# Query blocks of 496 and 351 columns, sixteen pairs weighted on GpSimd, and a new order of TensorE's work in a two-layer graph kernel

## The chip, the cores and the metric

The kernel runs on one core of a Trainium2 chip. The time is device microseconds of one launch. Engines are called as in the profile: PE is TensorE's matrix multiplication, PEld its loading of weights, DVE is VectorE, ACT is ScalarE, POOL is GpSimd, SP is the engine that issues most transfers.

## What is computed

3327 nodes with 128 channels pass two layers. Layer 0 is a graph convolution with a batch norm; layer 1, which takes nearly all of the time, is an attention that runs once for each of the 128 channels d:

```python
q = (x @ Wq.T).reshape(d, n, h)      # d = 128, n = 3327, h = 8
k = (x @ Wk.T).reshape(d, n, h)
v = (x @ Wv.T).reshape(d, n, h)
a = jnp.einsum('dnh,dmh->dnm', q, k) * scale
a = a + spatial_encoding + edge_encoding   # both are adj
a = jax.nn.softmax(a, axis=2)
out = jnp.einsum('dnm,dmh->dnh', a, v)
out = out.reshape(n, h * d)
return out @ Wo.T
```

So there are 128 attentions of 3327 queries against 3327 keys with only 8 features each, and the adjacency matrix is added twice to each score.

## The kernel before, in words

Everything is float32. Layer 0 and the preparation of layer 1 come first. Then the function `attention` works through 32 iterations (index `i`) of four channels each (`G = 4`). An iteration goes over the query blocks (index `y`), and each block over 13 steps (index `s`). Keys lie in 26 chunks of 128; a chunk is on the partitions and the queries of the block are the columns.

The unit of work is a pair: one chunk of keys and one half of the four channels, thus two channels. `product` (its matmul is L725) computes the scores of a pair with two matmuls of 32 rows each: the pair's half decides whether they use the first two or the last two of the array's four row groups. The result fills a tile `s` of two PSUM banks; there are three such tiles. A pair is then finished in one of two ways:

- plain: `add` on DVE (L818) adds the adjacency tile `at` into one of three places of `d`; later one exponential on ACT (L856) does all of `d`, issued one step later as `late`.
- weighted: `weighted` takes the exponential on ACT straight from PSUM (L828), and POOL multiplies it by exponentials of the adjacency values (L831, tile `wt`, read from the stored array `wd`).

A block has 52 pairs and each step handles four of them: three plain and one weighted in most steps, two and two in the last one. That makes 38 plain and 14 weighted pairs. `WC` is the first chunk that is weighted, and `pairs(s)` gives the pairs of a step.

The weights of the softmax are multiplied with v by `weigh` (L604): the stationary operand has 128 rows and 9 columns (8 features and a column of ones for the sum), and the two channels of a pair use two of the four column groups, again chosen by the half. This is done `LAG = 3` steps after the scores, by `second`. The program shows one such matmul as two instructions in the profile (two passes over the same columns). The output `av` takes one PSUM bank; there are two, in turns for the blocks.

All engines run in the order in which the program issues, so the order of calls in the loop over the steps is the order of TensorE's queue. Before, a step puts there: the score of the weighted pair, the score of the first plain pair, `second(0)` (pairs 0 and 1 of the old step), the scores of the other two pairs, and `second(1)` (pairs 2 and 3). `step()` moves on the end of a block, `finish`: a copy of `av` (L612), four transposes (L619), the division, the transfer to memory. `beside` puts in pieces of later or earlier work that use the other `av` bank: the projections of q, k and v for later channels (L196), two turns (L257) and a product (L265) of the output for earlier ones. `more_weights` prepares, in the first iteration only, the adjacency exponentials of the next blocks; the first `EARLY` blocks are prepared before the attention begins. `loads` fetches the next iteration's q, k and v, with a sorting copy on POOL (L180).

Of the kernel before, what the change touches and what calls it, by code (L numbers as in the profile page):

```python
# [18 lines left out]
N = 3327  # L19
# [3 lines left out]
NC = 26  # L23
T = N * D
NP = NC * P
NB = 512
G = 4
EPS = 1e-5
HALF = 0.5 / math.sqrt(D)
SAFE = 30.0  # L30
SU = NC // 2
WC = 19
CH = 4 * NP // D
NG = D // G
EARLY = 3

# [6 lines left out]
def tile_two_layer_gnn(  # L45
# [20 lines left out]
        mybir.EngineType.Pool, mybir.EngineType.SP,  # L66
    }))
    blocks = [(n0, min(NB, N - n0)) for n0 in range(0, N, NB)]

    const = ctx.enter_context(tc.tile_pool(name="const", bufs=1))  # L70
    dram = ctx.enter_context(tc.tile_pool(name="dram", bufs=1, space=DRAM))
# [42 lines left out]
    FROM = [3 * SU] + [LAG + 1] * (NG - 1)  # L114
# [171 lines left out]
    with tc.tile_pool(name="l0", bufs=1) as l0, tc.tile_pool(  # L286
# [125 lines left out]
        for c in range(NC):  # L412
# [16 lines left out]
            i = c - 2 * NQ - 5  # L429
            if 0 <= i < NQ - 2 and 4 * i + 4 <= c:  # L430
                spread(i)
        weights = []
        for y, (n0, w) in enumerate(blocks[:EARLY]):
            a = ap.tile([P, 7 * NB], F32, name="a")
            a7 = a.rearrange("p (c n) -> p c n", c=7)
            nc.sync.dma_start(a7[:, :, :w], adjr[:, WC:, n0 : n0 + w])
            weights.append((a7, n0, w))

# [170 lines left out]
    def finish(rp, av, d0, n0, w):  # L609

        avs = rp.tile([P, NB], F32, name="avs")
        nc.vector.tensor_copy(avs[:, :w], av[:, :w])  # L612
        yield

        J = 4 if w == NB else 3
        R = w // J
        pt = av.rearrange("p (j q) -> p j q", j=4)
        for j in range(J):
            nc.tensor.transpose(  # L619
                pt[:R, j, :], avs[:, j : j + (R - 1) * J + 1 : J], ident  # L620
            )
        yield
        pv = pt.rearrange("p j (b h) -> p b j h", h=32)
        ri = rp.tile([P, G, 4], F32, name="ri")

        nc.vector.tensor_scalar(ri[:R, :, :J], pv[:R, :, :J, H], 1e-30, None, ALU.max)  # L626
        nc.vector.reciprocal(ri[:R, :, :J], ri[:R, :, :J])  # L627
        o = rp.tile([P, G, 4, H], F32, name="oq")
        nc.vector.tensor_tensor(  # L629
            o[:R, :, :J, :],  # L630
            pv[:R, :, :J, :H],
            ri[:R, :, :J].unsqueeze(3).to_broadcast([R, G, J, H]),
            ALU.mult,
        )
        yield
        nc.sync.dma_start(
            attb[bass.ds(d0, G), n0 : n0 + w, :].rearrange(
                "b (p j) h -> p b (j h)", j=J
            ),
            o[:R, :, :J, :].rearrange("p b j h -> p b (j h)"),  # L640
        )
# [10 lines left out]
    def attention():  # L652


        with tc.tile_pool(name="adj", bufs=4) as ap, tc.tile_pool(
# [17 lines left out]
            if True:  # L673
                steps = [
                    (i, y, s)
                    for i in range(NG) for y in range(len(blocks)) for s in range(SU)
                ]

                def at(i):
# [2 lines left out]
                def pairs(s):  # L682


                    last = s == SU - 1
                    plain = [(j // 2, j % 2) for j in range(3 * s, 3 * s + 3 - last)]
                    rest = [(WC + s // 2, 1 - s % 2)]
                    return plain, rest + ([(NC - 1, 0)] if last else [])


                wanted, have = [], {}
                for x, (i, y, s) in enumerate(steps):
                    n0, w = blocks[y]
                    for c, _ in pairs(s)[0]:
                        if (0, i, y, c // 2) not in have:
                            have[0, i, y, c // 2] = None
                            wanted.append((x, 0, i, y, c // 2))
                    c = pairs(s)[1][0][0]
                    if (1, i, y, c) not in have:
                        have[1, i, y, c] = None  # L700
                        wanted.append((x, 1, i, y, c))

                def fetch(x):
                    while wanted and wanted[0][0] <= x:
                        _, kind, i, y, c = wanted.pop(0)
                        n0, w = blocks[y]
                        if kind:
                            a = wp.tile([P, NB], F32, name="wt")
                            nc.sync.dma_start(a[:, :w], wd[c - WC, :, n0 : n0 + w])
                        else:  # L710
                            a = ap.tile([P, 2, NB], F32, name="at")
                            n = min(2, WC - 2 * c)
                            nc.sync.dma_start(
                                a[:, :n, :w], adjr[:, 2 * c : 2 * c + n, n0 : n0 + w]
                            )
                        have[kind, i, y, c] = a

                def product(i, y, c, half):
                    q, k, _ = sets[i % 2]
                    n0, w = blocks[y]  # L720
                    we = w + w % 2
                    p = psc.tile([P, 2, NB], F32, name="s")
                    for x in range(2):
                        rs = slice(64 * half + 32 * x, 64 * half + 32 * x + 32)
                        nc.tensor.matmul(  # L725
                            p[:, x, :we], k[rs, c, :], q[rs, n0 : n0 + we],
                            start=True, stop=True,
                        )
                    return p
# [4 lines left out]
                def more_weights(i, y, s):  # L734

                    k, phase = s // 3, s % 3
                    if i or y + 1 >= len(blocks) or y + 1 < EARLY or k > 3:
                        return
                    n0, w = blocks[y + 1]
                    c = WC + 2 * k  # L740
                    n = min(2, NC - c)
                    if phase == 0:
# [13 lines left out]
                def beside(i, y, s):  # L756


                    for j in [1, 2] if i == 0 else [i + 2] if i + 2 < NG else []:
# [2 lines left out]
                        hj = wk.tile([P, CH], F32, name="hj")  # L762
                        nc.sync.dma_start(hj, hd[:, j * CH : (j + 1) * CH])
                        extra.extend(projections(wk, hj, j, False, ov, low_half[:CH, 1:2]))
                    if s in (8, 11) and extra:
                        drive(extra[0])
                    if s in (9, 12) and extra:
                        drive(extra.pop(0))
                    if s in (7, 10) and extra:
                        drive(extra[0], avs2[(i * len(blocks) + y + 1) % 2])  # L770
                    if (y, s) == (2, 12) and i:
                        extra.extend(outputs(wk, i - 1))

                extra = []

                def second(part):

                    (i, y, s), es = waiting[0]
                    n0, w = blocks[y]
                    av = avs2[(i * len(blocks) + y) % 2]  # L780
                    ps = sum(pairs(s), [])
                    for j in (0, 1) if part == 0 else (2, 3):
                        c, half = ps[j]
                        for x in range(2):
                            weigh(
                                sets[i % 2], av, w, es[j][:, x, :w], 2 * half + x, c,
                                s == 0 and part == 0, s == SU - 1 and part == 1,
                            )
                    if part:
                        waiting.pop(0)  # L790
                        if s == SU - 1:
                            ending.append(finish(rp, av, at(i), n0, w))

                def step():
                    for g in ending[:1]:
                        if next(g, g) is g:
                            ending.pop(0)

                for x, (i, y, s) in enumerate(steps):
                    n0, w = blocks[y]  # L800
                    fetch(x + PRE)
                    k = x - i * SU * len(blocks) - FROM[i]
                    if k == 0 and i + 1 < NG:
                        pending = loads(sets[(i + 1) % 2], at(i + 1))
                        total = len(pending)

                    while pending and (total - len(pending)) * (SU * len(blocks) - FROM[i] - 4) <= k * total:
                        pending.pop(0)()
                    more_weights(i, y, s)
                    due = len(waiting) == LAG  # L810
# [11 lines left out]
                            SAFE / 2, p[:, :, :w], ALU.min, ALU.add,  # L822
                        )

                    def weighted(c, half):
                        f = fp.tile([P, 2, NB], F32, name="f")
                        p = product(i, y, c, half)
                        nc.scalar.activation(  # L828
                            f[:, :, :w], p[:, :, :w], AF.Exp, scale=2.0
                        )  # L830
# [4 lines left out]
                        )  # L835
                        es.append(f)

                    weighted(*rest[0])
                    if late is not None:
                        late()  # L840
                    add(0, product(i, y, *plain[0]))
                    if due:
                        second(0)
                    step()
                    add(1, product(i, y, *plain[1]))
                    if len(rest) > 1:
                        weighted(*rest[1])
                    else:
                        add(2, product(i, y, *plain[2]))
                    beside(i, y, s)  # L850
                    if due:
                        second(1)

                    def late(d=d, w=w, n=len(plain)):
                        flat = d[:, :n].rearrange("p j x n -> p (j x) n")[:, :, :w]
# [1 line left out]

                    waiting.append(((i, y, s), es))
                late()
                while waiting:  # L860
                    second(0)
                    step()
                    second(1)
                while ending:
                    step()
                for p, b in zip(outputs(wk, NG - 1), (0, 1, 0)):
# [4 lines left out]
    def attention_shifted():  # L871

        with tc.tile_pool(name="shq", bufs=1) as shp, tc.tile_pool(
# [11 lines left out]
            with tc.For_i(0, D, G) as d0:  # L885
# [3 lines left out]
                for b in range(G):  # L889
# [1 line left out]
                        sh[32 * b : 32 * b + 1],  # L891
                        sT[:, bass.ds((d0 + b if b else d0) * N, N)],
                    )
                for y, (n0, w) in enumerate(blocks):
                    we = w + w % 2
                    av = avs2[y % 2]
                    waiting = []
# [166 lines left out]
```

## Time and profile before

| | |
|---|---|
| median of 3 runs | 10516.94 us (10514.26 to 10520.51) |
| profiled execution | 10527.91 us, its span 10526.1 us |
| mean granted TensorE clock | 0.986 |
| first score of the attention begins | 280.4 us after the span's start |
| iterations begin | 280.4, 667.9, 984.3, ... 5431.4, ... 9875.1, 10188.9 us |
| a steady iteration | 317.4 us (5431.4 to 9875.1, divided by 14) |
| DMA | 163 GB/s in mean; queue of the transfers busy 56.3% |

The times of instructions come from one profiled execution, and the span runs from its first to its last instruction. In the groups of instructions, a line gives the source line, the engine, the operation, the tiles (written<-read), the shapes and the count, then the busy time in us and the mean duration in ns of one, and then the idle time of the engine just before them and who ended it. In the waits, a line says who waited for whom, the total in us, the number of times and the longest. In the timeline the columns are the start and the duration in us; equal instructions that follow each other without a gap are merged to one row (xcount). A matmul row's duration reaches to its modelled end, and matmuls overlap in the array; the distance between starts is the better measure.

### The profile page before, as it was taken

To read this page: it belongs to the slowest core of one execution; us is meant where nothing else is said; L and a number is where in the kernel's file an instruction comes from. 1 tells how busy PE (TensorE), PEld (TensorE's weight loads), DVE (VectorE), ACT (ScalarE), POOL (GpSimd) and SP (SyncE) were. 2 spreads that over 40 slices of the span, in tenths; PEclk is the share of its full clock that TensorE was granted. 3 is DMA by queue.
4 is the path that set the end of the run, shared out by engine and by line. 5 is a ranking of instruction groups with operands and counts; after the bars stand their busy time and mean duration, and the time that the engine had idled before them with its cause. 6 is when DMAs were issued, how large, how long until landed. Compare 5 with 4: busy or idle time off the path is not lost. (4 is left out here: it accounts for less than half of the span.)

```text
span 10526.1 us, 186778 instructions
## 1 busy us (share of the span) xinstructions
PE 9922.7 (94%) x72399; PEld 2813.8 (27%) x72399; DVE 9714.9 (92%) x9949; ACT 9948.5 (95%) x6200; POOL 7497.1 (71%) x3868
## 2 busy tenths in 40 slices
PE   7889999999999999999999999999999999999999
PEld 3222222222222222222222222222222222222222
DVE  5789999999999999999999999999999999999998
ACT  4889999999999999999999999999999999999998
POOL 0667777777777777777777777777777777777776
PEclk8899999999999999999999999999999999999999
DMA  7655555555555555555555555555555555555554
GB/s 241 192 168 163 157 168 165 163 162 160 162 166 165 164 162 157 161 170 163 160 162 157 165 170 165 160 158 163 164 169 163 162 163 158 165 165 167 156 152 128
DMA packets 1115761, 1731.67 MB, mean 165 GB/s; under 512 B 198350, under 2 KB 441932, under 8 KB 1107180
## 3 DMA queue, kind: packets, MB, share of 16 engines
q1 hardware_dynamic: 1110478, 1713.99, 56.3%
q8 instruction: 568, 9.31, 0.4%
q10 hardware_dynamic: 4350, 5.64, 0.2%
q14 instruction: 333, 2.73, 0.1%
q0 software_dynamic: 32, 0.00, 0.0%
HBM read 1618.76 MB, written 100.53 MB: 163 GB/s over the span
## 5 line engine op out<-in xcount | busy, mean ns | idle before, releaser
L818 DVE SCALAR_TENSOR_TENSOR d<-at,s 128x1024 f32<-128x1024 f32 x8512 | 9204.3, 1138 | 642.7 <-PE s L725 406.2
L831 POOL TENSOR_TENSOR f<-f,wt 128x1024 f32<-128x1024 f32 (+1 forms) x3136 | 6983.8, 2235 | 2619.1 <-ACT f L828 2572.0
L856 ACT ACTIVATE d<-d 128x3072 f32<-128x3072 f32 (+1 forms) x2912 | 7372.9, 2532 | 73.4 <-DVE d L818 70.5
L604 PE MATMUL av<-d,v 128*9 128x512 f32 x34048 | 5528.5, 569 | 0.1
L725 PE MATMUL s<-q,k 32*128 32x512 f32 x23296 | 4280.7, 482 | 505.7 <-DVE d L818 218.0
L725 PEld LDWEIGHTS s<-q,k 32*128 32x128 f32 x23296 | 1773.9, 182 | 5829.2 <-DVE d L818 3312.2
L828 ACT ACTIVATE f<-s 128x1024 f32<-128x1024 f32 (+1 forms) x3136 | 3014.8, 970 | 313.8 <-PE s L725 252.3
L604 PE MATMUL av<-f,v 128*9 128x512 f32 x12544 | 2864.0, 571 | 0.0
L604 PEld LDWEIGHTS av<-d,v 128*9 128x9 f32 x34048 | 630.7, 88 | 1381.6 <-issue 1265.4
L604 PEld LDWEIGHTS av<-f,v 128*9 128x9 f32 x12544 | 310.6, 88 | 52.9 <-issue 41.0
L180 POOL CAST k<-ks 128x256 fp32r<-128x256 f32 x434 | 284.2, 655 | 0.0
L416 PE MATMUL acc<-a,A 128*128 128x512 f32 (+1 forms) x364 | 151.3, 568 | 24.0 <-ACT A L350 23.3
L619 PEld LDWEIGHTS av<-ident,avs 128*128 128x128 f32 (+1 forms) x864 | 121.1, 208 | 179.9 <-issue 178.8
L226 POOL TENSOR_TENSOR o<-pf,o 104x512 fp32r<-104x512 f32 x124 | 160.4, 1293 | 9.9
L619 PE MATMUL av<-ident,avs 128*128 128x128 f32 (+1 forms) x864 | 163.8, 311 | 0.6 <-DVE avs L612 0.6
L225 POOL CAST o<-pf 104x512 fp32r<-104x512 f32 x124 | 75.8, 611 | 115.3 <-DVE pf L224 59.8
L612 DVE COPY avs<-av 128x512 f32<-128x512 f32 (+1 forms) x224 | 144.2, 644 | 2.8 <-PE av L604 2.8
L423 DVE TENSOR_REDUCE amax<-a 128x1 f32<-128x3327 f32 x26 | 93.7, 3610 | 37.7 <-DMA a<-in_adj 37.7
L416 PEld LDWEIGHTS acc<-a,A 128*128 128x128 f32 x364 | 68.8, 192 | 108.8 <-issue 84.4
L420 ACT ACTIVATE junk<-a 128x3327 bf16<-128x3327 f32 x26 | 77.4, 2977 | 6.6 <-DMA a<-in_adj 6.5
L389 POOL TENSOR_TENSOR sq<-wk 128x512 f32<-128x512 f32 x2 | 2.1, 1040 | 102.3 <-PE aside L390 102.3
L629 DVE TENSOR_TENSOR oq<-av,ri 128x128 f32<-128x128 f32 (+1 forms) x224 | 64.1, 286 | 7.7
(120 smaller groups left out, 952.0 us busy)
## 6 DMA issues: line engine op xcount, KB each, us to landing
at<-in_adjT SPq DMA_DIRECT2D x1728, 512.0 KB
wt<-wd SPq DMA_DIRECT2D x1344, 256.0 KB
at<-in_adjT SPq DMA_DIRECT2D x288, 255.0 KB
ks<-kT SPq DMA_DIRECT2D x496, 104.0 KB
q<-qT SPq DMA_DIRECT2D x496, 104.0 KB
at<-in_adjT SPq DMA_DIRECT2D x192, 256.0 KB
a<-in_adj SPq DMA_DIRECT2D x26, 1663.5 KB
wt<-wd SPq DMA_DIRECT2D x224, 127.5 KB
```

The source lines that it names most:

```text
L180: nc.gpsimd.tensor_copy(k[:, c : c + n, half * 64 : half * 64 + 64], ks.bitcast(F32).rearrange("g (p c) -> g c p", c=NC)[:, c : c + n, :],)
L226: nc.gpsimd.tensor_tensor(o[:CH, 1], f[:CH], o[:CH, 0].bitcast(F32), ALU.subtract)
L416: nc.tensor.matmul(acc[i][:, :w], A[:, c, :], a[:, n0 : n0 + w], start=(c == 0), stop=(c == NC - 1),)
L423: nc.vector.tensor_reduce(amax[:, c : c + 1], a[:, :N], AX.X, ALU.max, apply_absolute_value=True)
L604: nc.tensor.matmul(av[32 * b : 32 * b + H + 1, :w], tiles[2][:, b, c, :], e, start=first, stop=last,)
L612: nc.vector.tensor_copy(avs[:, :w], av[:, :w])
L619: nc.tensor.transpose(pt[:R, j, :], avs[:, j : j + (R - 1) * J + 1 : J], ident)
L725: nc.tensor.matmul(p[:, x, :we], k[rs, c, :], q[rs, n0 : n0 + we], start=True, stop=True,)
L818: nc.vector.scalar_tensor_tensor(d[:, j, :, :w], have[0, i, y, c // 2][:, c % 2, :w] .unsqueeze(1).to_broadcast([P, 2, w]), SAFE / 2, p[:, ...
L828: nc.scalar.activation(f[:, :, :w], p[:, :, :w], AF.Exp, scale=2.0)
L831: nc.gpsimd.tensor_tensor(f[:, :, :w], f[:, :, :w], have[1, i, y, c][:, :w].unsqueeze(1).to_broadcast([P, 2, w]), ALU.mult,)
L856: nc.scalar.activation(flat, flat, AF.Exp, scale=2.0)
```

## The change

The queries are cut into six blocks of 496 and one of 351 instead of six of 512 and one of 255 (`QB`, `qblocks`); layer 0 keeps its own blocks. One more chunk of keys is weighted (`WC` 18 for 19), so that a block has 36 plain and 16 weighted pairs; steps 4, 8 and 12 (`DOUBLE`) take two of each kind, all others three plain and one weighted. The pairs of a step are dealt out in turn from the two lists (`kinds`), each with its half. Before the attention the weights of two blocks instead of three are prepared, in three pieces of 331 columns.

On TensorE, the score of a step's first weighted pair is issued at the end of the step before (`first`, `coming`). `second` now takes one pair at a time: pair 0 before the first plain score, pairs 1 and 2 between the first and the second plain score, pair 3 after that. `step()` stands between pairs 1 and 2. In `beside`, the second projection of a block moves by one step. Places where only `blocks` became `qblocks` are left out here.

```diff
 NP = NC * P
 NB = 512
+QB = 496
 G = 4
 EPS = 1e-5
 HALF = 0.5 / math.sqrt(D)
 SAFE = 30.0
 SU = NC // 2
-WC = 19
+WC = 18
 CH = 4 * NP // D
 NG = D // G
-EARLY = 3
+DOUBLE = (4, 8, 12)
+EARLY = 2
 
...
     }))
     blocks = [(n0, min(NB, N - n0)) for n0 in range(0, N, NB)]
 
+    qblocks = [(n0, min(QB, N - n0)) for n0 in range(0, N, QB)]
+
     const = ctx.enter_context(tc.tile_pool(name="const", bufs=1))
...
             if 0 <= i < NQ - 2 and 4 * i + 4 <= c:
                 spread(i)
         weights = []
-        for y, (n0, w) in enumerate(blocks[:EARLY]):
+        w = -(-EARLY * QB // 3)
+        for n0 in range(0, EARLY * QB, w):
             a = ap.tile([P, 7 * NB], F32, name="a")
-            a7 = a.rearrange("p (c n) -> p c n", c=7)
+            a7 = a.rearrange("p (c n) -> p c n", c=8)
             nc.sync.dma_start(a7[:, :, :w], adjr[:, WC:, n0 : n0 + w])
             weights.append((a7, n0, w))
...
         nc.vector.tensor_copy(avs[:, :w], av[:, :w])
         yield
 
-        J = 4 if w == NB else 3
+        J = 4 if w == QB else 3
         R = w // J
...
             if True:
                 steps = [
                     (i, y, s)
-                    for i in range(NG) for y in range(len(blocks)) for s in range(SU)
+                    for i in range(NG) for y in range(len(qblocks)) for s in range(SU)
                 ]
 
...
                 def pairs(s):
 
 
-                    last = s == SU - 1
-                    plain = [(j // 2, j % 2) for j in range(3 * s, 3 * s + 3 - last)]
-                    rest = [(WC + s // 2, 1 - s % 2)]
-                    return plain, rest + ([(NC - 1, 0)] if last else [])
+                    return kinds[s]
+
+                kinds = []
+                for s in range(SU):
+                    j, k = (sum(len(x[i]) for x in kinds) for i in range(2))
+                    n = 2 if s in DOUBLE else 1
+                    kinds.append((
+                        [(x // 2, x % 2) for x in range(j, j + 4 - n)],
+                        [(WC + x // 2, 1 - x % 2) for x in range(k, k + n)],
+                    ))
 
 
                 wanted, have = [], {}
                 for x, (i, y, s) in enumerate(steps):
-                    n0, w = blocks[y]
+                    n0, w = qblocks[y]
                     for c, _ in pairs(s)[0]:
                         if (0, i, y, c // 2) not in have:
                             have[0, i, y, c // 2] = None
                             wanted.append((x, 0, i, y, c // 2))
-                    c = pairs(s)[1][0][0]
-                    if (1, i, y, c) not in have:
-                        have[1, i, y, c] = None
-                        wanted.append((x, 1, i, y, c))
+                    for c, _ in pairs(s)[1]:
+                        if (1, i, y, c) not in have:
+                            have[1, i, y, c] = None
+                            wanted.append((x, 1, i, y, c))
 
                 def fetch(x):
                     while wanted and wanted[0][0] <= x:
                         _, kind, i, y, c = wanted.pop(0)
-                        n0, w = blocks[y]
+                        n0, w = qblocks[y]
                         if kind:
                             a = wp.tile([P, NB], F32, name="wt")
...
                         hj = wk.tile([P, CH], F32, name="hj")
                         nc.sync.dma_start(hj, hd[:, j * CH : (j + 1) * CH])
                         extra.extend(projections(wk, hj, j, False, ov, low_half[:CH, 1:2]))
-                    if s in (8, 11) and extra:
+                    if s in (8, 12) and extra:
                         drive(extra[0])
-                    if s in (9, 12) and extra:
+                    if s == 9 and extra or s == 0 and (y or i) and begun:
                         drive(extra.pop(0))
-                    if s in (7, 10) and extra:
-                        drive(extra[0], avs2[(i * len(blocks) + y + 1) % 2])
+                        begun.pop()
+                    if s in (7, 11) and extra:
+                        begun.append(1)
+                        drive(extra[0], avs2[(i * len(qblocks) + y + 1) % 2])
                     if (y, s) == (2, 12) and i:
                         extra.extend(outputs(wk, i - 1))
 
-                extra = []
-
-                def second(part):
-
+                extra, begun = [], []
+
+                def second(j):
+
+                    if not due:
+                        return
                     (i, y, s), es = waiting[0]
-                    n0, w = blocks[y]
-                    av = avs2[(i * len(blocks) + y) % 2]
+                    n0, w = qblocks[y]
+                    av = avs2[(i * len(qblocks) + y) % 2]
                     ps = sum(pairs(s), [])
-                    for j in (0, 1) if part == 0 else (2, 3):
-                        c, half = ps[j]
-                        for x in range(2):
-                            weigh(
-                                sets[i % 2], av, w, es[j][:, x, :w], 2 * half + x, c,
-                                s == 0 and part == 0, s == SU - 1 and part == 1,
-                            )
-                    if part:
+                    c, half = ps[j]
+                    for x in range(2):
+                        weigh(
+                            sets[i % 2], av, w, es[j][:, x, :w], 2 * half + x, c,
+                            s == 0 and j < 2, s == SU - 1 and j >= 2,
+                        )
+                    if j == 3:
                         waiting.pop(0)
                         if s == SU - 1:
                             ending.append(finish(rp, av, at(i), n0, w))
@@ -796,15 +810,21 @@
                         if next(g, g) is g:
                             ending.pop(0)
 
+                def first(x):
+
+                    i, y, s = steps[x]
+                    return product(i, y, *pairs(s)[1][0])
+
+                coming = first(0)
                 for x, (i, y, s) in enumerate(steps):
-                    n0, w = blocks[y]
+                    n0, w = qblocks[y]
                     fetch(x + PRE)
-                    k = x - i * SU * len(blocks) - FROM[i]
+                    k = x - i * SU * len(qblocks) - FROM[i]
                     if k == 0 and i + 1 < NG:
                         pending = loads(sets[(i + 1) % 2], at(i + 1))
                         total = len(pending)
 
-                    while pending and (total - len(pending)) * (SU * len(blocks) - FROM[i] - 4) <= k * total:
+                    while pending and (total - len(pending)) * (SU * len(qblocks) - FROM[i] - 4) <= k * total:
                         pending.pop(0)()
                     more_weights(i, y, s)
...
                             SAFE / 2, p[:, :, :w], ALU.min, ALU.add,
                         )
 
-                    def weighted(c, half):
+                    def weighted(c, p):
                         f = fp.tile([P, 2, NB], F32, name="f")
-                        p = product(i, y, c, half)
                         nc.scalar.activation(
                             f[:, :, :w], p[:, :, :w], AF.Exp, scale=2.0
                         )
@@ -835,21 +854,23 @@
                         )
                         es.append(f)
 
-                    weighted(*rest[0])
+                    weighted(rest[0][0], coming)
                     if late is not None:
                         late()
+                    second(0)
                     add(0, product(i, y, *plain[0]))
-                    if due:
-                        second(0)
+                    second(1)
                     step()
+                    second(2)
                     add(1, product(i, y, *plain[1]))
+                    second(3)
                     if len(rest) > 1:
-                        weighted(*rest[1])
+                        weighted(rest[1][0], product(i, y, *rest[1]))
                     else:
                         add(2, product(i, y, *plain[2]))
+                    if x + 1 < len(steps):
+                        coming = first(x + 1)
                     beside(i, y, s)
-                    if due:
-                        second(1)
 
                     def late(d=d, w=w, n=len(plain)):
                         flat = d[:, :n].rearrange("p j x n -> p (j x) n")[:, :, :w]
@@ -857,10 +878,11 @@
 
                     waiting.append(((i, y, s), es))
                 late()
+                due = True
                 while waiting:
-                    second(0)
+                    for j in range(4):
+                        second(j)
                     step()
-                    second(1)
                 while ending:
                     step()
```

## The prediction

> **What bounds the kernel now.** I read the busy table first, then the groups by shape, the waits, and last the timeline of TensorE alone.
>
> ```profile
> PE 9922.7 (94%) x72399; PEld 2813.8 (27%) x72399; DVE 9714.9 (92%) x9949; ACT 9948.5 (95%) x6200; POOL 7497.1 (71%) x3868
> ```
> Three engines stand above 90%, so the table alone doesn't name a limit: PE's share counts pipelined ends.
>
> ```profile
> L818 DVE SCALAR_TENSOR_TENSOR d<-at,s 128x1024 f32<-128x1024 f32 x7296 | 8417.5, 1213 | 474.6 <-PE s L725 270.4 <-issue 98.4 <-ACT d L856 23.7
> L856 ACT ACTIVATE d<-d 128x3072 f32<-128x3072 f32 x2304 | 6398.3, 2777 | 60.4 <-DVE d L818 59.1 <-ACT f L828 0.2
> L828 ACT ACTIVATE f<-s 128x1024 f32<-128x1024 f32 x2688 | 2753.2, 1032 | 239.1 <-PE s L725 211.8 <-POOL k L180 12.6 <-POOL f L831 7.2
> ```
> One step of a 512-wide block costs ACT one 2.78 and one 1.03 us exponential. Their ends overlap a little: in the trace the weighted exponentials of following steps start 3.56 us apart, and a block of 13 steps takes 47 to 49 us. DVE's three additions start 1.13 us apart, 3.39 us. So ACT sets the step, with DVE just behind.
>
> ```profile
> PEld s L725 <- DVE d L818: 3312.2, 4433, 6.4
> PEld s L725 <- ACT f L828: 1197.0, 1922, 11.8
> ACT f L828 <- PE s L725: 252.3, 380, 7.6
> ```
> The scores wait for a free PSUM tile (emptied by DVE or ACT), hardly the reverse. TensorE has spare time; how much must come from its own timeline. First 512 columns, then 255:
>
> ```profile
> 5004.75 0.51 PE L725 MATMUL s<-q,k 32*128 32x512 f32 x4
> 5005.18 0.60 PE L604 MATMUL av<-d,v 128*9 128x512 f32 x2
> 5005.62 0.60 PE L604 MATMUL av<-d,v 128*9 128x512 f32 x2
> 5006.16 0.90 PE L725 MATMUL s<-q,k 32*128 32x512 f32 x4
> ```
> ```profile
> 10487.41 0.39 PE L725 MATMUL s<-q,k 32*128 32x256 f32 x4
> 10487.72 0.39 PE L604 MATMUL av<-d,v 128*9 128x255 f32 x2
> 10487.94 0.38 PE L604 MATMUL av<-d,v 128*9 128x255 f32 x2
> 10488.27 0.38 PE L725 MATMUL s<-q,k 32*128 32x256 f32 x2
> ```
> Read the starts. Four scores of four different row groups start together, and 0.43 us later weighting begins. Four weightings of different column groups run side by side (the other two rows, av<-f, start within 0.02 us), but each is two passes, the second 0.43 to 0.44 us after the first; the next scores start 0.54 us after that. Over all such transitions of the trace the medians are, for 512 / 255 columns: score to weighting 430 / 318 ns, pass to pass 434 / 220, weighting to score 542 / 328. Two score groups of two followed by weighting still need 430: half a group costs as much as a whole one.
>
> A step needs two such alternations, 2 x 1.406 = 2.81 us of the 3.56. That is the reserve.
>
> **The change, part by part.**
>
> Widths. Seven blocks of 3327 columns in all before and after, and every cost above is a constant plus columns, so totals do not move. Slopes from the two widths: score 0.4375 ns a column, pass 0.833. At 496 / 351 columns: 423 / 360, 421 / 300, 529 / 408 ns; one alternation 1.373 / 1.068 us.
>
> Two more pairs on GpSimd per block: 2 x 7 x 32 = 448 pairs. DVE loses 448 x 1.138 = 510 us. POOL gains 448 x 2.235 = 1001 us, 8500 in all. ACT trades a share of a long exponential (about 0.78 us) for one of 0.97: +85 us. All three lie beside TensorE if that becomes the limit, as it does below; uncovered, only ACT's +85 would count. The one additional block of early weights is four exponentials of 1.15 us in the first iteration, and one weighted load more and one plain load fewer per block on SP's queue are the same bytes; both are hidden by the same margin. The second projection of a block moves by a step: product at step 11, copy at 12, its DMAs at step 0 of the next block, behind that step's loads on SP. Its rows are loaded an iteration later, and its PSUM tile is wanted at step 3, so nobody waits for it.
>
> New order. Per step TensorE's queue now holds: weighting j0 | score plain 0 | weighting j1, j2 | score plain 1 | weighting j3 | score plain 2 (or the second weighted one) and the next step's first score. Three alternations instead of two, and two of the three weighting groups are only two wide. What does a narrow group cost? No row shows one for av; the nearest is layer 0, where one matmul fills the array and nothing runs beside it:
>
> ```profile
> 61.28 0.60 PE L360 MATMUL aside<-ident,A 128*128 128x128 f32 x4
> 61.71 5.75 PE L416 MATMUL acc<-a,A 128*128 128x512 f32 x14
> 67.30 0.60 PE L360 MATMUL aside<-ident,A 128*128 128x128 f32 x4
> ```
> Twelve passes of 512 and two of 255 fill 61.71 to 67.30: 0.43 us per 512-column pass, as with four in flight. So a pass costs 0.43 however few share it (the other bound, half, is a rival below). Three alternations: 4.12 us at 496, 3.20 at 351.
>
> Halves. Which half of the array a pair uses decides what runs side by side. Writing out the halves of the new lists, the last score of a step and the next step's first have the same half in 10 of 13 steps, and j1 and j2 the same half in the three steps with two weighted pairs. Before, every neighbouring pair was opposite. The start of the attention holds the one place where the same row group is used twice without a wait:
>
> ```profile
> 280.66 0.70 PE L725 MATMUL s<-q,k 32*128 32x512 f32 x5
> 280.97 0.39 PE L725 MATMUL s<-q,k 32*128 32x512 f32 x1
> ```
> The second product of the first pair (280.66) and that of the third (280.97) are in one row group, 0.31 us apart; by the slope 0.30 at 496, 0.24 at 351. Bounds: 0, and 0.42 (a whole score slot); I take the row. A weighting group of equal halves needs two more passes, 0.84 / 0.60 us.
>
> Sum of a block, 496: 10 x (4.12 + 0.30) + 3 x (4.12 + 0.84) = 59.1 us; 351: 10 x 3.44 + 3 x 3.80 = 45.8. An iteration: 6 x 59.1 + 45.8 = 400.4.
>
> Other TensorE work per iteration. The seven block ends transpose between j1 and j2 and split that group: two passes more, 0.42 + 0.53, then 3 x 0.12 and 0.20 to the next weighting: 1.51 us (1.27 at 351), 10.3. Six projections, 0.513 + 0.522 each: 6.2. The output part: two turns of 0.62 and a product of 1.92: 3.2. Together 19.7, iteration 420.1 us, against 317.4 now.
>
> Does anything else reach 4.42 us a step? ACT 3.5 and DVE 3.3 at 496 do not. A PSUM tile is reused after three products: the addition of plain 0 ends some 1.6 us after its product starts, and the tile is wanted 2.7 us after it; the first exponential has about 4 us. The double steps queue two weighted exponentials and a shorter third on ACT within 4.96 us. The weighting of j3 waits for GpSimd work of three steps ago, 13 us, where a product takes 2.4. I find no wait.
>
> Total: 32 x 420.1 = 13443; before the first score 280.4; the end after the last regular iteration 20; the first iteration now takes 70 us longer than a steady one (start-up 11, the rest waits for additions), of which I keep half, 35. Span 13778, execution 13780 with the 1.8 us around the span. The profiled execution, 10527.9, is 0.1% above the median of the runs; carried over: **13770 us**, +31%.
>
> One rule is weighed here. The changes of kind carry 3 x 339 ns of a step. The Trainium skill, TensorEngine Tiling, Performance Considerations, gives each matmul about 60 cycles of overhead, 25 ns at the 2.4 GHz that TensorE: Matmul & The Clock Gate states. If that were the whole price of a change, an alternation at 496 would be an estimated 1.12 us and the total about 11540. The same Tiling page, Key Properties, says that changing the tiling mode drains the engine, without a price; that speaks against an order with more changes. The rows price it, and they decide.
>
> **Rivals.**
>
> Narrow passes at half price. If a group of two needed half the pass time, four passes a step save 0.84 us (0.60 at 351), 416 x (6 x 0.84 + 0.60) = 2350 us: 11420. For it: no av group of two appears alone in the trace. Against: the layer 0 row.
>
> Not slower: ACT stays the limit. If score and narrow weighting groups ran side by side in the array so that the step's TensorE work stayed under 3.5 us, the new order would deliver the first score early, remove ACT's 252 us of waits for scores, and add 85: about 10350. Point of decision: TensorE 3.5 us a step instead of 4.4. Against: not one of the 4700 weighting-to-score transitions at 512 columns is under 533 ns.
>
> More waits than I see, from semaphores or late GpSimd products: up to the 250 us that ACT now waits for scores, and full-price serial scores, 2240 x 0.12 = 270. That is my upper end, 14280.
>
> **How the numbers follow.** Likeliest: TensorE-bound near 13770, chance 0.87. It spans 13100 (same-half scores costing nothing, 2240 x 0.29 = 650 less) to 14280. Cheap narrow passes 0.09; ACT-bound 0.03; otherwise beyond 14280. The range is the likeliest case's own. About 0.2% is what a measurement here can tell from no change: faster 0.03, same 0.01, slower 0.96.
>
> **What would show it.** Right: weighted exponentials about 4.4 us apart in 496-wide blocks, a block 59 to 62 us; ACT near 73% (10033 of 13778) with its waits mainly for s; PEld's 3312 us of waits for DVE mostly gone; av groups of two still 0.42 between passes; same-half score pairs 0.30 apart. Wrong: a step near 3.5 us with ACT still above 93%, av passes 0.2 us apart, or TensorE still idling for DVE.

## The result, and the profile after

The changed kernel takes 13509 us (median of 4 runs, 13507 to 13516), the kernel before 10518 us beside it: a ratio of 1.2845, 95% interval 1.2823 to 1.2868. The forecast of 13770 (13100 to 14280) held; it was 1.9% too high.

First the busy table and the chain that ended last, of the changed kernel:

```profile
PE 13381.4 (99%) x72399; PEld 3320.0 (25%) x72399; DVE 9703.3 (72%) x9501; ACT 10425.8 (77%) x6652; POOL 8435.7 (62%) x4316
```
```profile
PE 98%; ACT 1%; DMA 1%; DVE 0%; issue 0%; POOL 0%; ACTq 0%; DVEq 0%; POOLq 0%; SPq 0%
PE av L609 64%; PE s L736 30%; PE av L200 1%; PE av L624 1%; PE acc L420 1%; PE av L269 0%; ACT f L847 0%; PE av L261 0%; DMA q<-qT 0%; DVE d L838 0%; DMA xs<-in_x 0%; ACT A L354 0%; ACT junk L424 0%; DMA a<-in_adj 0%; PE aside L410 0%
```
The number of TensorE's instructions is the same, 72399, yet its busy time grew by 3459 us (9922.7 before), and the chain follows it through 98% of the span. The waits (who for whom, us in total, times, longest) have turned round:

```profile
DVE d L838 <- PE s L736: 3246.9, 5205, 2.8
ACT f L847 <- PE s L736: 2726.9, 2679, 8.0
PEld s L736 <- DVE d L838: 941.8, 1150, 6.8
PEld s L736 <- ACT f L847: 616.8, 762, 10.5
```
The line of the kernel before for DVE is this; those for the other two stand in the prediction:

```profile
DVE d L818 <- PE s L725: 406.2, 785, 2.3
```
ACT waited 252 us for scores before and 2727 now; DVE 406 and 3247. The opposite wait, scores for a tile that DVE must empty, fell from 3312 to 942 us.

The timeline of TensorE shows where the time lies; the columns are start and duration, and the starts are what to read. One step runs from 5009.09 to 5013.17; the score row at 5013.17 ends a step with equal halves:

```profile
5009.09 0.49 PE L736 MATMUL s<-q,k 32*128 32x496 f32 x4
5009.51 1.00 PE L609 MATMUL av<-d,v 128*9 128x496 f32 x4
5010.44 0.49 PE L736 MATMUL s<-q,k 32*128 32x496 f32 x2
5010.87 1.02 PE L609 MATMUL av<-d,v 128*9 128x496 f32 x8
5011.82 0.49 PE L736 MATMUL s<-q,k 32*128 32x496 f32 x2
5012.24 1.01 PE L609 MATMUL av<-f,v 128*9 128x496 f32 x4
5013.17 0.72 PE L736 MATMUL s<-q,k 32*128 32x496 f32 x4
5013.82 1.01 PE L609 MATMUL av<-d,v 128*9 128x496 f32 x4
```
A narrow group (x4: one pair, two passes of two matmuls) occupies 0.93 us, 5009.51 to 5010.44. The full one (x8: two pairs) occupies 0.95, 5010.87 to 5011.82. Half the work, the same time. At 5009.09 two scores of opposite halves go to the next weighting in 0.42 us; at 5013.17 two of equal halves need 0.65. The whole step from 5009.09 to 5013.17 takes 4.08, because its first pair of scores happens to be opposite; a step with equal halves takes 0.23 more.

And one middle group of equal halves:

```profile
5000.62 1.01 PE L609 MATMUL av<-d,v 128*9 128x496 f32 x4
5001.45 1.00 PE L609 MATMUL av<-f,v 128*9 128x496 f32 x4
5002.38 0.49 PE L736 MATMUL s<-q,k 32*128 32x496 f32 x2
```
Its four passes come one after the other, 1.76 us where opposite halves need 0.95.

### The profile page after: what moved, and what is told of

The parts are those of the page before. It is cut to its first block, busy times and chain, and to the rows that moved or that the text cites. A ratio compares the mean times of both kernels' runs of the same rounds, so it can differ in the third digit from the quotient of the medians.

```text
span 13513.8 us, 187751 instructions
## 1 busy us (share of the span) xinstructions
PE 13381.4 (99%) x72399; PEld 3320.0 (25%) x72399; DVE 9703.3 (72%) x9501; ACT 10425.8 (77%) x6652; POOL 8435.7 (62%) x4316
## 4 chain that ended last, share of the span: by engine, by line
PE 98%; ACT 1%; DMA 1%; DVE 0%; issue 0%; POOL 0%; ACTq 0%; DVEq 0%; POOLq 0%; SPq 0%
PE av L609 64%; PE s L736 30%; PE av L200 1%; PE av L624 1%; PE acc L420 1%; PE av L269 0%; ACT f L847 0%; PE av L261 0%; DMA q<-qT 0%; DVE d L838 0%; DMA xs<-in_x 0%; ACT A L354 0%; ACT junk L424 0%; DMA a<-in_adj 0%; PE aside L410 0%
## 5 line engine op out<-in xcount | busy, mean ns | idle before, releaser
L838 DVE SCALAR_TENSOR_TENSOR d<-at,s 128x992 f32<-128x992 f32 x8064 | 9171.8, 1144 | 3644.6 <-PE s L736 3246.9
L850 POOL TENSOR_TENSOR f<-f,wt 128x992 f32<-128x992 f32 (+1 forms) x3584 | 7934.9, 2229 | 4787.6 <-ACT f L847 4777.0
L877 ACT ACTIVATE d<-d 128x2976 f32<-128x2976 f32 (+1 forms) x2912 | 6989.9, 2400 | 78.1 <-DVE d L838 50.1
L609 PE MATMUL av<-d,v 128*9 128x496 f32 x32256 | 5903.8, 564 | 0.0
L847 ACT ACTIVATE f<-s 128x992 f32<-128x992 f32 (+1 forms) x3584 | 3376.6, 962 | 2834.4 <-PE s L736 2726.9
L736 PE MATMUL s<-q,k 32*128 32x496 f32 x23296 | 4707.9, 458 | 37.6 <-ACT f L847 24.1
L609 PE MATMUL av<-f,v 128*9 128x496 f32 x14336 | 3480.1, 564 | 0.0
L609 PEld LDWEIGHTS av<-f,v 128*9 128x9 f32 x14336 | 438.5, 89 | 1066.8 <-issue 957.0
L624 PE MATMUL av<-ident,avs 128*124 128x128 f32 (+1 forms) x864 | 164.9, 312 | 0.7 <-DVE avs L617 0.7
L617 DVE COPY avs<-av 128x496 f32<-128x496 f32 (+1 forms) x224 | 144.8, 646 | 3.9 <-PE av L609 3.9
```

The source lines that it names most:

```text
L609: nc.tensor.matmul(av[32 * b : 32 * b + H + 1, :w], tiles[2][:, b, c, :], e, start=first, stop=last,)
L624: nc.tensor.transpose(pt[:R, j, :], avs[:, j : j + (R - 1) * J + 1 : J], ident)
L736: nc.tensor.matmul(p[:, x, :we], k[rs, c, :], q[rs, n0 : n0 + we], start=True, stop=True,)
L838: nc.vector.scalar_tensor_tensor(d[:, j, :, :w], have[0, i, y, c // 2][:, c % 2, :w] .unsqueeze(1).to_broadcast([P, 2, w]), SAFE / 2, p[:, ...
L847: nc.scalar.activation(f[:, :, :w], p[:, :, :w], AF.Exp, scale=2.0)
L850: nc.gpsimd.tensor_tensor(f[:, :, :w], f[:, :, :w], have[1, i, y, c][:, :w].unsqueeze(1).to_broadcast([P, 2, w]), ALU.mult,)
```

## The experiments

Each ran beside the kernel before, whose median was 10511 to 10514 us. The theory: the order of TensorE's queue makes the whole loss, by three terms: a third change of kind per step with narrow groups, equal halves side by side, and split block ends. The rivals: the widths, the pairs on GpSimd, the score issued early.

**e1_widths: the widths alone.**

```diff
-                for i in range(NG) for y in range(len(blocks)) for s in range(SU)
+                for i in range(NG) for y in range(len(qblocks)) for s in range(SU)
```
(with `QB = 496`, and `qblocks` in all places of the attention; the rest is the kernel before)

> Widths of 496 and 351 alone, order, pairs and everything else as before. Theory (the order of TensorE's queue makes the whole loss): every cost is a constant plus columns and the blocks stay seven, so ACT still sets the step: 10520 us, within 30. Rival (the widths cost or bring something by themselves, through shapes or the last block): beyond 10490 to 10550, and well above 11000 if they had a share in the loss.

Measured: 10432 us, ratio 0.9923 (0.9910 to 0.9937). The widths have no share in the loss. They bring 0.8%, which the prediction had as nothing: outside the expected 30 us. The groups of ACT by shape say where it came from, first of the kernel before, then of this one (the number behind the bar's comma is the mean ns, then comes the idle time of ACT ahead of the group). They are shown for the weighted exponentials; the line of the wide blocks before stands in the prediction (239.1 us idle):

```profile
L828 ACT ACTIVATE f<-s 128x510 f32<-128x510 f32 x448 | 269.8, 602 | 74.7 <-PE s L725 40.5 <-POOL k L180 18.8
```
```profile
L831 ACT ACTIVATE f<-s 128x992 f32<-128x992 f32 x2688 | 2678.3, 1004 | 222.9 <-PE s L728 191.8 <-POOL k L183 13.9 <-POOL f L834 7.5
L831 ACT ACTIVATE f<-s 128x702 f32<-128x702 f32 x448 | 341.4, 762 | 21.9 <-PE s L728 19.3
```
ACT's idle time ahead of the narrow block's weighted exponentials falls from 75 to 22 us, that of the wide ones from 239 to 223. ACT is nearly as busy as before (9921 us against 9949).

**e2_old_order: the change without its order.**

```diff
-                    weighted(rest[0][0], coming)
+                    weighted(rest[0][0], product(i, y, *rest[0]))
...
-                    second(0)
                     add(0, product(i, y, *plain[0]))
+                    second(0)
                     second(1)
                     step()
-                    second(2)
                     add(1, product(i, y, *plain[1]))
-                    second(3)
...
-                    if x + 1 < len(steps):
-                        coming = first(x + 1)
                     beside(i, y, s)
+                    second(2)
+                    second(3)
```

> The changed kernel with TensorE's order and the pieces in beside put back as before; widths of 496 and 351, 16 weighted pairs in steps 4, 8, 12 and the smaller early weights stay. In the old order all neighbouring pairs of the new lists have opposite halves. Theory: ACT sets the step again and pays 448 shorter instructions more, about 85 us, and gets back part of its 252 us of waits for scores: 10450 to 10620 us, the 510 us off DVE bring nothing else. Rival (the second weighted pair in three steps starves ACT or GpSimd and has a share in the loss): above 10800.

Measured: 10441 us, 0.9931 (0.9918 to 0.9945), 9 us below the range that was expected. The pieces in `beside` are put back to their old steps as well. With the order put back the whole loss is gone, while 16 pairs, double steps and widths stay. DVE's busy time is 397 us less than with 14 pairs (9301 against 9698), and this buys nothing. That fits ACT as the engine that sets the step; the time is that of e1 within 10 us.

**e3_order_alone: the order without the rest** (`QB = 512`, `WC = 19`, `DOUBLE = (12,)`, `EARLY = 3` in the changed kernel).

> The new order alone: 512 and 255 columns, 14 weighted pairs, two of them in the last step only, early weights as before. Theory, from the distances between starts in the trace after: a single step 4.42 us at 512 and 2.68 at 255 columns, a double one 5.06 and 3.01 (12 of 13 steps have equal halves at the step's end, one has them in the middle group), an iteration 383.9 plus 19.8 of other work, 32 of them and 323 us around: 13240 us. It would carry 2720 of the 2990 us lost. Rival (the loss needs the sixteen pairs or the widths as well): below 12500.

Measured: 13278 us, 1.2630 (1.2610 to 1.2649), 38 us from the sum. The order alone makes 2765 us of the loss; the other 231 us between this kernel and the changed one come only when the sixteen pairs and the widths meet the new order, for they cost nothing in the old one (e2_old_order).

**e4_halves: three alternations without equal halves.**

```diff
-                        [(WC + x // 2, 1 - x % 2) for x in range(k, k + n)],
+                        [(WC + x // 2, x % 2) for x in range(k, k + n)],
```

> The changed kernel with the halves of the weighted pairs swapped (x % 2 for 1 - x % 2), so that the two scores at a step's end and the two pairs in the middle group are always opposite; three alternations and narrow groups stay. Theory: a single step falls from 4.31 to 4.09 us at 496, a double one from 4.93 to 4.09; iteration 379.9, total 12480 us, thus 1030 less than the changed kernel. Rival (equal halves cost nothing, only the narrow groups and the changes of kind do): 13510.

Measured: 12509 us, 1.1898 (1.1880 to 1.1916): 1000 us below the changed kernel, 29 from the sum. One expression that changes no amount of work is worth 1000 us. Its timeline has every pair of scores side by side (x4 in 0.42 to 0.43 us) and every middle group in 0.95:

```profile
5002.14 0.50 PE L736 MATMUL s<-q,k 32*128 32x496 f32 x4
5002.57 1.01 PE L609 MATMUL av<-d,v 128*9 128x496 f32 x4
5003.50 0.49 PE L736 MATMUL s<-q,k 32*128 32x496 f32 x2
5003.92 0.59 PE L609 MATMUL av<-d,v 128*9 128x496 f32 x2
...
5004.87 0.49 PE L736 MATMUL s<-q,k 32*128 32x496 f32 x2
5005.29 1.01 PE L609 MATMUL av<-f,v 128*9 128x496 f32 x4
5006.23 0.50 PE L736 MATMUL s<-q,k 32*128 32x496 f32 x4
```
The step from 5002.14 to 5006.23 takes 4.09 us, as summed.

**e7_end_moved: block ends that split no group.**

```diff
                     second(1)
-                    step()
                     second(2)
+                    step()
```

> The changed kernel with step() moved behind pair 2, so that the four transposes at a block's end no longer split the group of pairs 1 and 2; everything else as in the change. Theory: each of 224 block ends saves two passes, 0.94 us at 496: 200 us, 13310 us. Rival (the transposes hide in TensorE's other work): 13510.

Measured: 13314 us, 1.2661 (1.2641 to 1.2680): 195 us below the changed kernel, where 200 were expected. Four transposes between two pairs of one group cost two passes more, and nothing hides them when TensorE has no slack.

**e10_one_split: one moved call in the old order** (edit against e2_old_order).

```diff
                     add(1, product(i, y, *plain[1]))
+                    second(2)
                     if len(rest) > 1:
...
                     beside(i, y, s)
-                    second(2)
                     second(3)
```

> The kernel with the old order (16 pairs, 496 and 351) and one call moved: second(2) goes ahead of the step's last score, so that the second weighting group becomes two narrow ones with a score between them. Three alternations, neither the early score nor equal halves, the block's end not splitting a group. Theory: 4.09 us a step at 496 and 3.17 at 351, 13.4 us of other work an iteration, 373.5; total 12280 us, 1840 above the old order from one moved call. Rival (the early score, or the interplay with DVE, is what costs, and the third change of kind hides in TensorE's slack): below 11000.

Measured: 12369 us, 1.1763 (1.1745 to 1.1781), 1928 us above e2_old_order and 89 above the sum, which stays unexplained. This is the smallest form of the fault: no early score, no equal halves, no split end, one third change of kind with two narrow groups.

```profile
PE 12198.8 (99%) x72399; PEld 2942.9 (24%) x72399; DVE 9677.3 (78%) x9501; ACT 10135.6 (82%) x6652; POOL 8459.2 (68%) x4316
```
TensorE goes from 9837 us busy in e2_old_order to 12199, with the same matmuls.

**e5_two_groups and e6_two_groups_14: the early score with two full groups.**

```diff
                     second(0)
-                    add(0, product(i, y, *plain[0]))
                     second(1)
                     step()
-                    second(2)
+                    add(0, product(i, y, *plain[0]))
                     add(1, product(i, y, *plain[1]))
+                    second(2)
                     second(3)
```

> The changed kernel with only the middle of the step regrouped: the first score still comes at the end of the step before, but pairs 0 and 1 are weighted together before the first plain score and pairs 2 and 3 together after the second one; two alternations, no narrow groups; widths, 16 pairs, halves as in the change (equal at a step's end in 10 of 13). Theory: TensorE needs 2.75 us a step at 496 and 0.22 more where halves are equal, below ACT's 3.4 to 3.5, so the whole loss goes: 10200 to 10500 us, at or below the 10441 of the old order, the more the earlier score removes ACT's 262 us of waits for scores. Rival (issuing the score a step ahead is itself harmful): above 10600.

> As the regrouped kernel, but with 14 weighted pairs, two of them in the last step alone. Theory: ACT has 448 short exponentials less (85 us) but DVE stands at 3.3 us a step in nearly all steps, close to ACT: 10200 to 10450, within 100 of the 16-pair version. Rival (the 16 pairs are what makes the early score pay, by giving DVE slack): over 100 us above it.

Measured: 10552 us, 1.0032 (1.0020 to 1.0045), with 16 pairs, and 10743 us, 1.0214 (1.0200 to 1.0228), with 14 pairs (`WC = 19`, `DOUBLE = (12,)`). Both miss. Two groups take back nearly the whole loss, so the theory of the loss stands, but against the old order this arrangement costs 111 us with 16 pairs and 310 with 14 (e1_widths). The waits of the 16-pair version:

```profile
ACT d L877 <- DVE d L838: 222.8, 511, 0.7
DVE d L838 <- ACT f L847: 204.3, 559, 1.6
...
ACT f L847 <- PE s L736: 81.2, 66, 7.8
```
and of e2_old_order, for comparison:

```profile
ACT f L844 <- PE s L736: 261.6, 605, 7.7
ACT d L872 <- DVE d L835: 12.7, 33, 0.7
```
ACT does get its weighted score sooner: its waits for s fall from the 262 us of e2_old_order to 81. But ACT now waits 223 us (13 in e2_old_order) for the sums of DVE, so the wait has moved. The line `DVE d <- ACT f` does not mean that DVE waits for ACT: these additions begin 107 ns (median) after the end of their own score, as those do that the trace puts down to the score (112 ns). DVE waits for a score. From the second iteration on, 968 of the 986 us that the additions wait stand ahead of the first addition of a step (490 in e2_old_order). Its score starts 0.64 us (median) after its PSUM tile came free, directly behind the weighting of two pairs, 0.95 us, which this order puts ahead of it. This points to a place in TensorE's queue again, and not to a tile that is held longer: from the start of a weighted score to the end of its exponential it is 1.90 us here and 2.04 in e2_old_order (medians). No run moves the early score and the first plain score apart, so the share of each in the 111 us stays open. The 16 pairs are worth 190 us here and only 9 the other way in the old order (e1_widths against e2_old_order); they leave DVE more time. That was given as the rival of e6.

**e8_504 and e9_492: why the widths brought 80 us** (`QB = 504` and `492` in e1_widths).

> As the widths alone, but 504 and 303 columns. Open: why 496 and 351 alone brought 80 us. In those traces ACT is as busy as before, but idle 245 instead of 314 us ahead of its weighted exponentials, 47 of the 69 less in the narrow block. Theory (a narrow block of 255 is too short for TensorE's constants and ACT waits there; the wider it is, the less): between, about 10475. Rival (a full bank of 512 columns is slow by itself): the whole gain, about 10430.

> As the widths alone, but 492 and 375 columns. Theory (waits in the narrow block): only 41 us of idle are left there to ACT at 351 columns, so little more is to be had: 10400 to 10435. Rival (the gain goes on with every column taken from the wide blocks, 5 us a column): below 10415 and going on.

Measured: 10466 us, 0.9952 (0.9939 to 0.9966), with 504 and 303 columns; 10518 us, 1.0004 (0.9995 to 1.0013), with 492 and 375. The first lies between as expected and speaks against a full bank being slow. The second fits neither expectation: the gain is gone. ACT's idle time in the wide blocks of 492 grew instead of falling:

```profile
L831 ACT ACTIVATE f<-s 128x984 f32<-128x984 f32 x2688 | 2651.7, 994 | 268.1 <-PE s L728 241.2 <-POOL k L183 11.8 <-POOL f L834 8.1
```
268 us against 223 at 496: a wide block of 492 takes as long as one of 496, 46.66 and 46.63 us in the mean from its first weighted exponential to the next block's. The traces show where the time goes. The end of a wide block transposes four times 124 columns at 496 and four times 123 at 492 (first e1_widths, then e9_492):

```profile
L622 PE MATMUL av<-ident,avs 128*124 128x128 f32 x768 | 141.0, 306 | 0.0
L622 PE MATMUL av<-ident,avs 128*123 128x128 f32 x768 | 223.3, 413 | 0.0
```
Neighbouring transposes start 118 ns apart with 124 columns and 224 ns apart with 123 (medians). The step that holds them takes 3.75 us from weighted exponential to weighted exponential, against 3.47 at 496, while most other steps are 0.02 to 0.03 us shorter; and ACT waits 37 us in all for the next score there, against 1 us. That is about 0.3 us in each of the 192 wide blocks, 58 of the 86 us between the two runs. So shorter waits in the narrow block explain a part of the gain at 496, dearer transposes most of its loss at 492, and a rest stays open. No run changes the transposes alone. The best measured version is e1_widths, 10432 us.

## Why the prediction was right

- **What bounds it.** ACT before, TensorE after: the chain and the reversed waits show the second, and e2_old_order, where less work for DVE buys nothing, fits the first. The rival in which ACT stays the limit fails: weighted exponentials start 4.30 us apart (median, 4.4 forecast), a wide block takes 60.5 us (59 to 62), and ACT has 2.7 ms of waits for scores.
- **Price of an alternation.** The rows of before gave 1.373 us at 496. After: score to weighting 420, pass to pass 420, weighting to score 529 ns behind a full group (as predicted) and 516 behind a narrow one, 13 less.
- **Narrow passes.** Predicted 0.42 us from the layer 0 row, measured 420 ns in the median of 7100 of them; the rival of half price falls. e10_one_split shows the consequence by itself, +1928 us.
- **The rule that was weighed.** The estimate of 11540 us by 60 cycles for each matmul is 1970 us too low. That a change of kind costs more than its columns agrees with the drain that the Trainium skill names (TensorEngine Tiling, Key Properties); no run here shows that the cost is a drain. One figure of that paragraph does not follow from the prediction's own slopes: by these the columns of an alternation at 496 make 1.043 of its 1.373 us, so a step's changes carry 3 x 330 ns and not 3 x 339. The forecast does not use it.
- **Equal halves.** Predicted 0.30 us for a second score in the same row group, measured 0.33, but the weighting after it starts 0.32 us later and not 0.42. Together 0.65 where 0.73 was summed; this is the mis-sized term. 60 such pairs an iteration at 496 columns, and 10 at 351, make 5.7 us, and the 13 ns behind narrow groups another 2.3. That is the difference of the iteration: 412.2 us measured (from first scores 14 iterations apart), 420.1 summed, times 32 about 250 of the 261 us that the forecast was too high. e4_halves measures the whole term, with the double steps, at 1000 us; the prediction's terms give 1194.
- **Block ends.** The prediction's terms make 205 us of the split (0.95 us at 496 and 0.71 at 351, 32 times seven blocks); 195 measured (e7_end_moved).
- **Widths at nothing.** Wrong by 81 us, in the sense of a gain: ACT waits less in a wider last block, and a part stays open (e8_504 and e9_492). It did not matter in the sum, where TensorE sets the time and the sum of the columns is the same.
- **Other engines.** GpSimd at 8436 us (8500 predicted) and DVE stay beside. ACT is at 77%, not 73%: it stands at 10426 us in the table, against 9952 in e2_old_order with the same instructions, since the ends of exponentials in close succession overlap there and count once, and here stand apart (the durations add up to 10594 and 10678 us). For the same reason the 510 us that DVE was to lose do not show in its busy time, 9703 us against 9715; its durations add up to 461 us less. The first iteration kept half of its additional time, 447 us against 412. That half was assumed without a reason, so this term came out by luck.
- **Where the loss comes from**, by the runs, 2996 us against the 10513 of before that ran beside e1 to e4: widths and pairs together -72 (e2_old_order), the third change of kind with narrow groups +1928 (e10_one_split), split ends and all that the early score adds or saves +140 (the rest up to e4_halves), equal halves +1000.

## What to carry to other kernels

Count TensorE's groups, not its matmuls: in these runs matmuls that share the array ran together only where they stood next to each other in the queue and used different row or column groups, so a call moved between two of them doubled their time with no instruction added (0.95 us for a weighting group of two pairs, 0.93 for one pair by itself). Before work is put between groups to feed another engine, price a change of kind from the distances between starts, and compare the step's sum with the engine that now sets the step. A score issued early for one engine can push the score of another back in the queue, as in e5_two_groups: look at who waits for that one.

## What the runs showed of the hardware that was not expected

A score in the same row group as the one ahead of it starts 330 ns later at 496 columns, but the following weighting then starts 316 ns after it instead of 420 (medians). A weighting group of two leads to the next score in 516 ns, one of four in 529. Transposes of 123 columns start 224 ns apart, those of 124 only 118 (e9_492, e1_widths). In the other runs and blocks, too, an odd number of columns (85, 101, 117, 125) gives 168 to 222 ns and an even one (126, 128) 120 to 121; these four odd numbers belong to the last block, whose transposes take every third column instead of every fourth, so that only 123 against 124 shows the number by itself. The mean granted clock was 0.986 in the profile before, 0.990 to 0.993 in the other profiles in which TensorE is 94 to 96% busy, and 0.996 in those in which it is 99% busy.
